# Three pacing constants of a two-layer perceiver: first layers, context sums and routed experts

## The chip, the cores and the metric

The kernel runs on one core of a Trainium2 chip. The metric is the device time of one execution in microseconds; the median of three runs stands for a kernel. One further execution was taken with the hardware profiler, and all views of the trace are of that one. The engines are called by the names of the profile: PE is the matrix engine, PEld its weight loads, DVE the vector engine, ACT the scalar engine, POOL the general engine, SP the engine whose queue issues most DMAs.

## The reference

32 sequences of 64 rows and 256 columns (`x`) attend to 32 contexts of 1601 rows and 256 columns (`ctx_1024`). All arithmetic is float32 but for a ternary last stage.

```python
# first layer
x = x + layernorm(x) @ W1.T + (sum of ctx over its rows) @ W2.T / 1601 + b
x = x + self_attention(layernorm(x))            # 16 heads, a slope bias, 64 x 64 scores
x = x + moe(layernorm(x))                       # shared silu-gated part, and routed experts:
    # routing over all 2048 rows; the rows that routing picks come from flat_idx, and the
    # routed results are added at out[flat_idx], which names only rows 0 to 7
# second layer
x = x + cross_attention(layernorm(x), ctx)      # 16 heads, 64 queries, 1601 keys
x = x + recurrent_block(layernorm(x))           # conv, gated scan, silu-gated part
x = x + ternary_mlp(layernorm(x))
```

`flat_idx` holds expert numbers, so that the routed experts change only eight rows of the first tile, but their counts and groups depend on the routing of all rows.

## The kernel before

The 2048 rows are 16 tiles of 128 rows (two sequences each). They are taken in the order 1 to 15, then 0; `pos` is the place in that order. The cross attention is the backbone: a tile has four halves (two sequences by two groups of 128 channels), and a half four **pieces** of 384 keys (the last has 449). There are 256 pieces, `t` = 0 to 255, and every one issues the same operations in the same order: `column_scores` (L705, the PE products into `s`, then the exponentials into `pt` on ACT), `values` of the next half (`vps` on PE, copied to `vau` on DVE, L667), other work at **place 0**, `row_scores` (L671: products into `r` on PE, the two maxima into `mx` on DVE, L685), `weighted` (L744), `keys` (`kps`), other work at **place 1**. `s` and `r` share one pool of two PSUM tiles, so the products into `s` of the next piece wait until DVE has reduced `r` of this one. All other products go through `mm_tile` (L69), three PSUM tiles in rotation.

Everything else is written as generators that issue a few instructions and yield. A list `plan` (L1128 to L1139) says when each advances; engines then execute in the order of issue, and no scheduler changes it. An entry is `Steps(gen, t0, t1, n, place)`: `n` steps are spread evenly from piece `t0` to piece `t1`, by the rule

```python
while self.gen is not None and self.done * (self.t1 - self.t0) <= (now - self.t0) * self.n:
    self.step()
```

With place 0 the steps run at place 0; with place 2 at both, where place 1 counts as half a piece later; with place 3 at most one step runs in a piece, at place 0 if the step before it ended on ACT's work and else at place 1. At `t1` what is left runs at once. The entries are:

- `first_layer(pos)` (`layer0`, L253): 25 steps, at most one a piece, so about 25 pieces. Step 4 is the first product's input, 8 the query and key products (`q`, `k`), 10 the scores, 11 to 14 the softmax, 16 to 19 the attention's output, 22 to 24 the shared gated part (`su`, `sv`, `so`). It ends in `x3`, the residue, and a column of `logits`.
- `sums(pos, 3)` (`context_sums`, L241): four loads of half a context (`part`, one buffer, SP's queue) and a sum over each on ACT (L236). Three steps lie between a load and its sum, 17 steps in all.
- `queried(pos)` (`query`, L619): the queries of the cross attention, from `x3`.
- `second_layer(pos - 1)` (recurrent block and ternary part): 33 steps from piece `16 * pos + 1` on. Two of them are under way at any time.
- `last_routed()` (`routed`, L423): 78 steps at both places. Step 1 to 3 is the softmax of `logits`; 4 to 7 rank the groups and 8 to 11 the experts (`ranks`, L451, DVE alone: lines L461 to L469); 12 and 13 select and count (`r_cnt`, with one product `cnt_ps`); 14 to 22 load the expert weights and gather the eight rows (`a_ps`, `asb`); 23 to 71 run through eight groups of 512 assignments, each by six steps: DVE makes `ohw` (L561), PE transposes it into `tpo` (L566) and ACT copies that to `ohT` (L568), PE makes `gps` (L574), twice, with a gate on ACT and DVE (`hr`, L229 to L232), and PE adds up `h_ps` (L582); 72 to 78 produce the eight rows.

The routed experts need the logits of all tiles, so they start after the last first layer, and `queried(15)` needs their result: it starts at 229. Half 60, the first of the last tile, has its row scores from piece 235 on. After piece 255 the rest of the last two second layers runs without any backbone.

Of the kernel before, what the change touches and what calls it, by code (L numbers as in the profile page):

```python
# [9 lines left out]
F32 = mybir.dt.float32  # L10
# [5 lines left out]
P = 128  # L16
NB = 32
S = 64
D = 256
# [25 lines left out]
def perceiver_kernel(ctx: ExitStack, tc: tile.TileContext, a: dict, out: bass.AP):  # L45
# [4 lines left out]
    work = ctx.enter_context(tc.tile_pool(name="work", bufs=2))  # L50
# [170 lines left out]
    def mm2(o, lhsT, rhs):  # L221

        for c in range(2):
            nc.tensor.matmul(o, lhsT=lhsT(c), rhs=rhs(c), start=(c == 0), stop=(c == 1))  # L224
# [16 lines left out]
    def context_sums(ti, wait):  # L241

        csum = sums_tile(ti)
        for b in range(2):
            for c in range(2):
                part = load_part(2 * ti + b, c)
                for _ in range(wait):
                    yield
                summed(ti, csum, b, c, part, part)
                yield  # L250
        return csum

    def layer0(ti, csum, k=0, soon=False):  # L253
# [160 lines left out]
        yield  # L414
        o = mm_tile([P, D], f"so_{ti}")
        mm2(o, lambda c: m[:, c, :], lambda c: w_s2[:, c, :])
        x3 = work.tile([P, D], F32, tag="x3", name=f"x3_{ti}", bufs=3)
        nc.vector.tensor_tensor(x3, o, x, ALU.add)
        yield
        return x3  # L420
# [659 lines left out]
    x3, x4, csums = {}, {}, {}  # L1080

    def sums(pos, wait):
        csums[pos] = yield from context_sums(order[pos], wait)

    def first_layer(pos, k=0):
        x3[pos] = yield from layer0(order[pos], csums[pos], k)

    def queried(pos):
        yield from query(pos, x3[pos])

    def second_layer(pos):
        yield from tail(order[pos], x4[pos])

    def last_routed():
        yield from routed(x3[NT - 1])

    def first():

        csum = sums_tile(order[0])
        steps = layer0(order[0], csum, 0, True)  # L1100
        next(steps)
        yield
        next(steps)
        yield
        next(steps)
        junk = big.tile([P, L], F32, tag="part", name="junk", bufs=1)
        for b in range(2):
            yield
            summed(order[0], csum, b, 0, ctxs[b][:, 0, :], junk)
            nc.vector.tensor_reduce(csum[:, 1, b:b + 1], ctxs[b][:, 1, :], AX.X, ALU.add)  # L1110
        csums[0] = csum
        yield
        x3[0] = yield from steps
        yield from query(0, x3[0])
# [13 lines left out]
    plan = [Steps(first_layer(2), 0, 14, 26, 2)]  # L1128
    for pos in range(1, NT):
        if pos > 2:  # L1130
            t0 = 15 * (pos - 3) + 2 + 4 * (pos == 3)
            plan.append(Steps(first_layer(pos), t0, t0 + 28 - 4 * (pos == 3), 28, 3))
            if pos > 3:
                plan.append(Steps(sums(pos, 3), t0 - 16, t0 - 1, 17, 0))
        if pos < NT - 1:
            plan.append(Steps(queried(pos), 16 * (pos - 1) + 2, 16 * (pos - 1) + 10, 6, 0))
        plan.append(Steps(second_layer(pos - 1), 16 * pos + 1, 16 * pos + 30, 33, 3))
    plan.append(Steps(last_routed(), 210, 229, 78, 2))
    plan.append(Steps(queried(NT - 1), 229, 234, 6, 2))  # L1139

    ET = mybir.EngineType
    with tc.manual_schedule(engines={ET.PE, ET.DVE, ET.Activation, ET.Pool}):
# [40 lines left out]
        for h in range(4 * NT):  # L1183
            pos, q = divmod(h, 4)
# [77 lines left out]
```

## Time and profile before

| What | Value |
|---|---|
| median of three runs | 2245.73 us (2244.09 to 2249.22) |
| the profiled execution | 2246.56 us |
| its span, first to last instruction | 2244.8 us |
| PE busy | 2116.0 us, 94% |
| PEld busy | 1563.1 us, 70% |
| DVE busy | 1370.1 us, 61% |
| ACT busy | 933.5 us, 42% |
| POOL busy | 325.8 us, 15% |
| mean granted clock of PE | 0.973 |
| HBM read | 117.70 MB, 53 GB/s over the span |

The span is the time between the first and last instruction of the profiled execution; 1.8 us of its 2246.56 us lie around it. A piece is found in the trace by the products of line L714, the first of its column scores: piece 0 starts at 110.69 us, piece 212 at 1799.78 us, piece 255 at 2165.28 us. A view of waits says which engine stood, on what, and for how long in total; a view of windows gives the busy time of each engine in a stretch and the clock that PE was granted in it, 1.00 being full speed.

### The profile page before, as it was taken

The page shows a single profiled execution, that of the slowest core. Times are in us where ns is not written, and L with a number is a line of the kernel's source. Part 1 is how long each engine was busy: PE and PEld are TensorE (multiplying, and loading weights), DVE is VectorE, ACT ScalarE, POOL GpSimd, SP SyncE. Part 2 cuts the span into 40 slices and gives each one's busy share as a digit, 9 for nine tenths or more (in the row PEclk, how much of TensorE's full clock was granted, in tenths as well). Part 3 has the DMA queues.
Part 4 walks back from the last instruction along what each step waited for, and adds up shares of the span by engine and source line. Part 5 has one row for each costly group of instructions (what it writes and reads, how often), then busy time and mean ns, then how long its engine had stood idle before and what let it go on. Part 6 is the DMA issues. An engine that isn't in the chain of part 4 may idle for free. (4 is left out here: it accounts for less than half of the span.)

```text
span 2244.8 us, 70681 instructions
## 1 busy us (share of the span) xinstructions
PE 2116.0 (94%) x32015; PEld 1563.1 (70%) x32031; DVE 1370.1 (61%) x2926; ACT 933.5 (42%) x1653; POOL 325.8 (15%) x545
## 2 busy tenths in 40 slices
PE   5799999999999999999999999999999988899984
PEld 3476677777677777777776777777777756677763
DVE  3466665666656666665656566665665676666554
ACT  3343444453535444444544444454434313334341
POOL 4111111111111111111111111111110100000011
PEclk8699999999999999999999999999999999999996
DMA  7322111011111111111111101111010011010000
GB/s 240 125 100 96 63 60 63 31 66 47 62 63 61 65 61 36 52 60 60 65 61 63 54 29 63 60 65 46 31 43 30 16 49 40 4 41 34 2 4 5
DMA packets 34763, 124.32 MB, mean 55 GB/s; under 512 B 3218, under 2 KB 16546, under 8 KB 34464
## 3 DMA queue, kind: packets, MB, share of 16 engines
q1 hardware_dynamic: 32608, 115.02, 14.8%
q8 instruction: 251, 4.11, 0.7%
q0 software_dynamic: 1296, 3.97, 0.5%
q10 hardware_dynamic: 560, 0.81, 0.1%
q14 instruction: 48, 0.39, 0.1%
HBM read 117.70 MB, written 2.10 MB: 53 GB/s over the span
## 5 line engine op out<-in xcount | busy, mean ns | idle before, releaser
L685 DVE TENSOR_REDUCE mx<-r 128x2 f32<-128x768 f32 (+1 forms) x512 | 483.8, 986 | 117.1 <-PE r L682 115.9
L726 ACT ACTIVATE pt<-s 128x768 f32<-128x768 f32 x512 | 393.6, 808 | 300.3 <-PE s L721 300.2
L224 PE MATMUL vps<-w_L_xattn_WvT,ctxT 128*128 128x128 f32 (+1 forms) x3328 | 443.8, 285 | 0.0
L650 ACT ACTIVATE kt<-kps,chv 128x384 f32<-128x384 f32 (+1 forms) x256 | 152.1, 594 | 673.7 <-PE kps L224 673.6
L224 PE MATMUL kps<-ctxT,w_L_xattn_WkT 128*128 128x384 f32 (+1 forms) x1024 | 415.3, 529 | 10.8 <-DMA ctxT<-ctxT 10.8
L224 PEld LDWEIGHTS vps<-w_L_xattn_WvT,ctxT 128*128 128x128 f32 (+1 forms) x3328 | 392.1, 189 | 31.1 <-issue 1.0
L667 DVE COPY vau<-vps 128x384 f32<-128x384 f32 (+1 forms) x320 | 154.5, 499 | 378.3 <-PE vps L224 378.0
L744 PEld LDWEIGHTS o<-pt,vau 128*32 128x32 f32 x12288 | 183.9, 110 | 147.7 <-issue 143.7
L682 PE MATMUL r<-kt,qbd 32*128 32x384 f32 (+1 forms) x2048 | 260.9, 552 | 3.2 <-DVE mx L685 1.6
L224 PEld LDWEIGHTS kps<-ctxT,w_L_xattn_WkT 128*128 128x128 f32 x1024 | 175.4, 191 | 111.2 <-issue 37.7
L721 PE MATMUL s<-qbd,kt 32*128 32x128 f32 x6656 | 234.2, 271 | 0.0
L744 PE MATMUL o<-pt,vau 128*32 128x64 f32 x12288 | 225.9, 221 | 2.5 <-ACT pt L726 2.5
L721 PEld LDWEIGHTS s<-qbd,kt 32*128 32x128 f32 x6656 | 222.0, 183 | 4.2
L682 PEld LDWEIGHTS r<-kt,qbd 32*128 32x128 f32 x2048 | 90.1, 184 | 50.4 <-issue 20.6
L714 PEld LDWEIGHTS <-onesb 3*128 3x128 bf16 x1024 | 28.5, 91 | 130.0 <-issue 127.8
L714 PE MATMUL s<-neg,onesb 3*128 3x384 bf16 (+1 forms) x1024 | 98.0, 345 | 17.4 <-DVE mx L685 17.3
L236 ACT ACTIVATE part<-part 128x1601 f32<-128x1601 f32 x60 | 92.5, 1542 | 7.5 <-DMA part<-ctxT 7.5
L761 DVE RECIPROCAL rs<-sums 128x128 f32<-128x128 f32 x64 | 60.6, 947 | 0.1
L302 POOL TENSOR_TENSOR kbd<-kT,mask 128x512 f32<-128x512 f32 x32 | 32.8, 1046 | 155.0 <-ACT kT L295 155.0
L224 PE MATMUL ff<-nT,w_fg 128*128 128x128 f32 x384 | 51.9, 287 | 1.0 <-ACT nT L873 1.0
L908 POOL TENSOR_SCALAR q_i<-h 128x1024 bf16<-128x1024 f32 x16 | 16.7, 1044 | 241.5 <-DVE h L905 189.6
L348 POOL TENSOR_TENSOR s<-s,mx 128x1024 f32<-128x1024 f32 x15 | 28.5, 1903 | 154.8 <-DVE mx L332 145.2
(342 smaller groups left out, 2501.3 us busy)
## 6 DMA issues: line engine op xcount, KB each, us to landing
ctxT<-ctxT SPq DMA_DIRECT2D x32, 1601.0 KB, 6.6
part<-ctxT SPq DMA_DIRECT2D x60, 800.5 KB, 4.4
x<-x SPq DMA_DIRECT2D x16, 128.0 KB, 3.6
out<-x SPq DMA_DIRECT2D x16, 128.0 KB, 1.7
w<-w SPq DMA_DIRECT2D x16, 128.0 KB, 2.2
sum_L_ffn_w1T<-L_ffn_w1T SPq DMA_DIRECT2D x4, 256.0 KB, 4.6
raw_L_ffn_w1T<-L_ffn_w1T SPq DMA_DIRECT2D x4, 256.0 KB, 3.8
sum_L_ffn_w2T<-L_ffn_w2T SPq DMA_DIRECT2D x4, 256.0 KB, 2.6
```

Source lines behind the costliest of these rows:

```text
L224: nc.tensor.matmul(o, lhsT=lhsT(c), rhs=rhs(c), start=(c == 0), stop=(c == 1))
L236: nc.scalar.activation(junk, src, AF.Copy, accum_out=csum[:, c, b:b + 1])
L302: nc.gpsimd.tensor_tensor(kbd[oc], kT[:, oc, :].rearrange("p (b k) -> p b k", b=2).unsqueeze(2).to_broadcast([P, 2, 4, S]), mask4.unsqueez ...
L650: nc.scalar.activation(kt[:, :n], o[:, :n], AF.Identity, bias=chv[:, hf.oc, BK2:BK2 + 1])
L667: nc.vector.tensor_copy(v[:kr, j0:j0 + n, 0:VW - 16].rearrange("p k (h d) -> p k h d", d=17)[:, :, :, 0:16], o[:kr, j0:j0 + n, :].rearrang ...
L682: nc.tensor.matmul(ps[i // 2][:, i % 2, :n], lhsT=qbd[r, hf.oc, hf.b].rearrange("p h q -> p (h q)"), rhs=hf.kt[k][r, :n], start=True, stop ...
L685: nc.vector.tensor_reduce(hf.mx[:, 2 * m:2 * m + 2, k], ps[m][:, :, :n], AX.X, ALU.max)
L714: nc.tensor.matmul(ps[i // 2][:, i % 2, :n * P], lhsT=onesb[r, :], rhs=hf.neg[r, :].unsqueeze(1).to_broadcast([3, n, P]), start=True, stop ...
L721: nc.tensor.matmul(ps[i // 2][:kr, i % 2, j * P:(j + 1) * P], lhsT=hf.kt[g][r, k0:k0 + kr], rhs=qbd[r, hf.oc, hf.b].rearrange("p h q -> p ...
L726: nc.scalar.activation(pt.rearrange("p i k c -> p i (k c)"), ps[m][:, :, :3 * P], AF.Exp)
L744: nc.tensor.matmul(hf.o[32 * c:32 * c + 32, m, :], lhsT=v[:kr, j, 17 * hd:17 * hd + 32], rhs=hf.pt[m][j][:kr, c // 2, c % 2 * S:c % 2 * S ...
L761: nc.vector.reciprocal(rs, t)
```

## The change

First layers start 14 pieces apart in place of 15. The sums of a tile take the 13 pieces before its first layer, but start at piece 7 at the earliest (for the fifth tile, `pos` 4, that is 7 to 15 in place of 1 to 16). The routed experts take the pieces 199 to 229 in place of 210 to 229. `x3` gets a fourth buffer. The first layer of `pos` 15 thereby starts at piece 170 in place of 182. No instruction is added or taken away.

```diff
-        x3 = work.tile([P, D], F32, tag="x3", name=f"x3_{ti}", bufs=3)
+        x3 = work.tile([P, D], F32, tag="x3", name=f"x3_{ti}", bufs=4)
...
-            t0 = 15 * (pos - 3) + 2 + 4 * (pos == 3)
+            t0 = 14 * (pos - 3) + 2 + 4 * (pos == 3)
             plan.append(Steps(first_layer(pos), t0, t0 + 28 - 4 * (pos == 3), 28, 3))
             if pos > 3:
-                plan.append(Steps(sums(pos, 3), t0 - 16, t0 - 1, 17, 0))
+                plan.append(Steps(sums(pos, 3), max(t0 - 14, 7), t0 - 1, 17, 0))
         if pos < NT - 1:
             plan.append(Steps(queried(pos), 16 * (pos - 1) + 2, 16 * (pos - 1) + 10, 6, 0))
         plan.append(Steps(second_layer(pos - 1), 16 * pos + 1, 16 * pos + 30, 33, 3))
-    plan.append(Steps(last_routed(), 210, 229, 78, 2))
+    plan.append(Steps(last_routed(), 199, 229, 78, 2))
     plan.append(Steps(queried(NT - 1), 229, 234, 6, 2))
```

## The prediction

> **What bounds the kernel now.** I read the page first, then windows over stretches of the backbone, then PE's waits in the stretches with holes, then windows of single pieces.
>
> ```profile
> PE 2116.0 (94%) x32015; PEld 1563.1 (70%) x32031; DVE 1370.1 (61%) x2926; ACT 933.5 (42%) x1653; POOL 325.8 (15%) x545
> ...
> PE   5799999999999999999999999999999988899984
> ```
>
> PE is busy nearly throughout, but for the start, the end, and three slices in the routed experts' stretch. The change keeps every instruction, so PE's work stays; only its holes, and time at a lowered clock, can move. Windows cut at piece starts (columns: PE, PEld, DVE, ACT and POOL busy, then granted clock, DMA share, GB/s):
>
> ```profile
> core 0: us, PE busy (x) PEld busy (x) DVE busy (x) ACT busy (x) POOL busy (x), PEclk, DMA share, GB/s
> 1783.18:1829.03 45.85, 35.81 (x488) 26.73 (x488) 38.66 (x107) 12.04 (x24) 3.62 (x10) 0.89 0.11 38
> ...
> 1852.36:1979.55 127.19, 114.59 (x1540) 81.81 (x1540) 78.81 (x175) 46.64 (x87) 8.23 (x16) 0.99 0.09 33
> ...
> 2003.73:2048.94 45.21, 44.81 (x713) 32.27 (x714) 29.34 (x70) 20.36 (x36) 3.28 (x7) 1.00 0.11 38
> 2083.59:2113.76 30.17, 30.17 (x484) 22.74 (x484) 15.54 (x30) 11.58 (x22) 2.31 (x5) 1.00 0.01 2
> ...
> 285.58:1783.18 1497.60, 1481.32 (x23311) 1101.64 (x23319) 938.67 (x1974) 668.98 (x1185) 222.63 (x356) 1.00 0.15 53
> ```
>
> The first row is pieces 210 to 213 (routed steps 1 to 13), the second 216 to 227 (the eight groups). The third is pieces 231 to 236 and the fourth 242 to 245: backbone and two second layers alone. The last, 180 pieces with first layers, has 16.3 us of hole in 1497.6. So what is to be had lies in the routed experts: 10.0 us of hole and 0.11 x 45.85 = 5.0 us of clock in the first row, 12.6 us of hole and about 1.7 of clock in the second. PE's waits in these two stretches:
>
> ```profile
> PE s L714 <- DVE mx L685: 7.9, 4, 6.0
> PE cnt_ps L503 <- DVE r_cnt L501: 2.1, 1, 2.1
> ```
>
> ```profile
> PE tpo L566 <- DVE ohw L561: 6.7, 5, 1.6
> PE gps L574 <- ACT ohT L568: 2.1, 3, 0.8
> PE h_ps L582 <- DVE hr L232: 2.1, 2, 1.8
> ```
>
> The first is DVE overloaded: rank operations are queued ahead of `mx`, and the next piece waits. The second is latency: a step's PE instruction waits for what the step just before it gave to DVE or ACT.
>
> **The eight groups (a gain).** Before, 78 steps over 19 pieces are 2.05 steps a place: after place j (0 at piece 210) `floor(2.0526 j) + 1` steps are done. So two steps share nearly every place. Which pairs share follows from the rule: up to step 37 an even step and the next (24-25, 28-29, 30-31, 34-35, 36-37), from 39 on an odd one and the next (41-42, 47-48, 53-54, 59-60, 65-66). In a group, `ohw` is made in step 23+6g, `tpo` in 24+6g, `gps` in 25+6g, the last `hr` in 28+6g, `h_ps` in 29+6g. That gives three shared `tpo`-`gps`, two shared `hr`-`h_ps` and five shared `ohw`-`tpo`: just the counts 3, 2 and 5 of the waits. The stalls are thus pairs, at 1.34, 0.7 and 1.05 us.
>
> After, 2.6 steps a piece give `floor(1.3 j) + 1`, and three places in ten hold two: (35,36), (48,49), (52,53), (65,66), (70,71) among the groups. Two are `ohw`-`tpo` (2.7 us), one `tpo`-`gps` (0.7), two `hr`-`h_ps` (2.3 with the odd 0.6 us one that this view also has): 5.7 us. Before, with three smaller waits (0.7, 0.6, 0.4), it was 12.2-12.6. **Gain 6.5.** The clock fell to 0.67 over 1882.82 to 1888.00, behind the 1.76 us wait for `hr`, 1.7 us; one such wait has an even chance of coming again: **gain 0.9**. Bounds for the two together: 3 (all pairs that remain cost the longest wait) and 12.
>
> **The ranking (no gain).** Steps 1 to 14 move from pieces 210-213 to 199-204, six pieces in place of four. I had expected more room there, but the phases of the second layers repeat every 16 pieces, and 199-204 has the phases of 231-236, the third row. Free DVE time there is 45.2 - 29.3 = 15.9 us; in 242-245, the phases of 210-213, it is 30.2 - 15.5 = 14.6 us. The routed steps added 38.66 - 15.54 = 23.1 us of DVE, and step 14 (clearing and filling `r_z`) 1.6. Overflow before 8.5, after 54.0 - 45.2 = 8.8. The single pieces 232 to 236, below a row of before's stall:
>
> ```profile
> 1812.59:1819.30 6.71, 6.34 (x52) 5.71 (x52) 6.37 (x16) 1.51 (x2) 0.00 (x0) 0.58 0.00 1
> ...
> 2014.06:2020.78 6.72, 6.72 (x108) 4.92 (x108) 6.51 (x17) 2.09 (x3) 0.87 (x2) 1.00 0.01 2
> 2020.78:2026.82 6.04, 6.04 (x104) 4.11 (x105) 4.07 (x11) 2.29 (x5) 2.40 (x5) 1.00 0.01 4
> 2026.82:2033.42 6.60, 6.55 (x105) 4.25 (x106) 2.72 (x4) 4.70 (x6) 0.00 (x0) 1.00 0.00 0
> 2033.42:2041.55 8.13, 7.82 (x133) 5.32 (x134) 5.22 (x13) 4.41 (x8) 0.00 (x0) 1.00 0.48 168
> 2041.55:2048.94 7.39, 7.35 (x120) 5.30 (x120) 4.76 (x12) 3.29 (x7) 0.00 (x0) 1.00 0.10 41
> ```
>
> Piece 200 (like 232) has DVE full already: `mx` ends 0.6 us ahead of the next piece. Step 3 (1.8 us of DVE) at its place 0 makes a stall of 1.2. Step 4 (1.4) is carried over, 201 takes steps 5 and 6 (2.8) ahead of `mx`: its copy of `vau` ends 2.3 us late, stall 2.9. 202 takes step 7 (1.4) and 8 (3.2): 1.8. Steps 9 and 10 (6.1) at its place 1 delay the copy of `vau` in 203, step 11 (3.1) follows ahead of `mx`: 5.1. In 204, step 12 (1.3), the round trip of `cnt_ps` (PE waits 2.5), and steps 13 and 14 ahead of `mx`: 2.2. Together 15.7. Each of the five stalls on `mx` ends some 0.5 us sooner, since the first scores need only the first of two reductions: 13.2. Before it was 10.0. **Loss 3.2**; bounds -5 (a gain: the overflow spread evenly, 8.8 less what is left over at the end) and 6.
>
> Here a rule speaks for the change: the Trainium skill, Perfetto Trace Analysis, section Optimization Strategy, says that stretches with different contended engines may gain by being interleaved. By it all 29 us of holes and clock would go, and the time be about 2217. But the rows show DVE's free time equal in both places. I take the rows.
>
> **The clock.** The row 1812.59 to 1819.30 was granted 0.58, after the 6.04 us wait, and 1819.30 to 1829.03 got 0.82 behind one of 2.14. The Trainium skill, TensorE: Matmul & The Clock Gate, Part 1, lets the clock halve after about 3.4 us of idleness. By that only the stall of 5.1 would lower it, 1.7 to 3.4 us lost; by the rows stalls from 1.8 us on can, up to 8. While DVE is the bound part of the loss hides under the waits for it. I take 3 (before 5.0), **gain 2**, bounds 0 lost to 8.
>
> **First layers 14 apart (about nothing).** Summed from the groups by line over 600 to 1500 us, a first layer brings some 11 us of DVE and 14 of PE: it brings more PE time than DVE time, so packing it denser does not overload DVE. What is new is that step 22 of one layer and step 8 of the next share place 0: `su`, `sv`, `k` and `q` ask for four PSUM tiles out of three. `q` waits until `su` is read; PE needs 2.1 us for `sv` and `k`, ACT's tanh and DVE's copy 0.8 after `su`. Covered; if DVE is behind, the nearest row is `su` waiting 0.7 us for a tile. I take **0.5 us** in all, bounds -2 and 15 (eleven pairs at 1.4). POOL (15% busy) takes its part of the moved steps under cover.
>
> **Sums, loads, `x3` (nothing).** Each tile's four loads (800.5 KB, 4.4 us to land) stay three steps ahead of their sums: 2.3 pieces, some 18 us, in place of 2.6; for `pos` 4 two pieces, 14 us. On SP's queue they pass the context loads (6.6 us to land), still inside. If a load came late, ACT would stand, and `pt` and PE behind it, at most a few us per tile. The routed weights (2.2 us to land) are loaded two steps ahead, now one and a half places rather than one. At most three `x3` live at a time in either kernel, so the fourth buffer ends no wait. After piece 229 nothing moves.
>
> **The sum.** -6.5 - 0.9 + 3.2 - 2.0 + 0.5 = -5.7. From the profiled 2246.56 that is 2240.9; the median stands 0.83 below that execution, so 2240.0.
>
> **The rivals.** *A, the holes vanish*: spreading lets DVE catch up between pieces, as it has slack in the mean (45.2 against 29.3). Then 10.0 + 5.0 of the ranking mostly go besides the 7.4 of the groups: -22, 2224. Against it: the full row of piece 232, and that steps come in pairs just at the ranks (9, 10). *B, PSUM at the eleven joint places*: `q` and `k` wait for `su` and `vps` behind a DVE that still copies `vau`. At 1.3 us per tile, +14 on the -5.7: 2254. It decides from 0.5 us per tile on. For it: `su` already waits 0.7 us for a tile here and there; against it: in 1497.6 us all waits make 16.3. *C, the change does little*: the groups' pairs cost more than counted and the ranking takes the gain: -1, 2245.
>
> **How the numbers follow.** A measurement of this kernel can tell about 0.2%, 4.5 us, from no change. The likeliest case with C in its upper part has 0.55, range 2233 to 2247: faster 0.32, same 0.22, slower 0.01. A has 0.2, all faster. B has 0.25: slower 0.22, same 0.03. The range 2226 to 2254 leaves out the lower part of A and the upper of B; faster and slower both being open, the likeliest case's own range is 2233 to 2247.
>
> **What would show it.** PE's waits of `tpo`, `gps` and `h_ps` should be 2, 1 and 2 times, some 5.5 us. `mx` should hold up `s` in pieces 200 to 204, 8 to 13 us, with a clock below 1 there. Pieces 205 to 228 should be nearly without holes. PE's hole before piece 199 should stay near 16 us per 1500. Waits of `q`, `k`, `su` or `so` at 0.5 us and more, a dozen of them, would be B; no wait on `mx` about piece 203 would be A; a wait on a DMA of `part` would refute the cover of the sums.

## The result and the profile after

| Kernel | median, us | ratio to before | 95% interval |
|---|---|---|---|
| before | 2246.13 | | |
| changed | 2250.02 | 1.0019 | 1.0012 to 1.0026 |

The change makes the kernel 3.9 us slower (2250.02 - 2246.13, 20 runs of each), 0.19%, clear of the noise. The profiled execution of the changed kernel took 2253.73 us, at the upper side of its runs: the rest from piece 252 on, the same instructions in both kernels, took 93.7 us in it at a mean granted clock of 0.71, and 91.1 us at 0.74 in that of before. So stretches of the backbone are compared here, not spans. First the page of the changed kernel:

```profile
span 2251.7 us, 70663 instructions
...
PE 2122.3 (94%) x32015; PEld 1566.7 (70%) x32031; DVE 1369.0 (61%) x2926; ACT 934.3 (41%) x1653; POOL 327.1 (15%) x545
...
PE   5799999999999999999999999999999899999984
```

The three weak slices of the routed experts have become one. PE, PEld, DVE, ACT and POOL have the same numbers of instructions as before. The windows of the changed kernel, cut at its own piece starts (PE, PEld, DVE, ACT and POOL busy, granted clock, DMA share, GB/s), are in this order pieces 16 to 194, 199 to 204 (the ranking), 205 to 209, 207 to 227 (the eight groups), and 0 to 251, the whole backbone up to its last half:

```profile
236.06:1681.23 1445.17, 1423.05 (x22290) 1057.34 (x22296) 906.96 (x1902) 646.07 (x1142) 226.26 (x357) 1.00 0.16 54
...
1712.62:1773.94 61.32, 49.06 (x705) 34.66 (x706) 50.75 (x147) 20.92 (x37) 3.84 (x10) 0.94 0.08 28
1773.94:1821.87 47.93, 47.40 (x608) 33.14 (x609) 25.93 (x50) 13.25 (x22) 3.14 (x5) 0.93 0.17 48
1796.33:1985.36 189.03, 183.30 (x2639) 133.00 (x2640) 116.83 (x258) 70.48 (x132) 14.10 (x27) 1.00 0.10 34
111.24:2157.99 2046.75, 1999.68 (x31051) 1476.52 (x31066) 1280.25 (x2731) 876.10 (x1546) 276.75 (x448) 1.00 0.15 51
```

The same for before, first pieces 16 to 194 and then the whole backbone:

```profile
235.52:1666.72 1431.20, 1414.93 (x22221) 1051.84 (x22229) 901.95 (x1890) 642.93 (x1136) 223.24 (x354) 1.00 0.16 54
...
110.69:2153.69 2043.00, 1996.36 (x31051) 1475.14 (x31064) 1281.27 (x2731) 875.25 (x1546) 275.54 (x448) 0.99 0.15 51
```

The backbone is 3.75 us longer (2046.75 - 2043.00), about what the medians say. In pieces 16 to 194 PE's holes (length less busy) grew from 16.3 to 22.1 us. In the ranking they are 12.3 us, 10.0 before; in the groups 5.7, 12.6 before. So the holes shrank in the routed part and grew under the first layers, and over the whole backbone they about cancel: 47.1 us, 46.6 before. The other 3.3 us of the loss are PE busy time (1999.68 - 1996.36), with the same instructions and a mean granted clock of 1.00 (0.99 before). Which part of the change costs them, the windows don't tell; the runs below do.

### The profile page after: what moved, and what is told of

Read it like the earlier page. It is cut to its first block, busy times and chain, and to the rows that moved or that the text cites. A ratio compares the mean times of both kernels' runs of the same rounds, so it can differ in the third digit from the quotient of the medians.

```text
span 2251.7 us, 70663 instructions
## 1 busy us (share of the span) xinstructions
PE 2122.3 (94%) x32015; PEld 1566.7 (70%) x32031; DVE 1369.0 (61%) x2926; ACT 934.3 (41%) x1653; POOL 327.1 (15%) x545
## 4 chain that ended last, share of the span: by engine, by line
PE 84%; DVE 9%; ACT 3%; issue 2%; POOL 1%; SPq 1%; DMA 0%; POOLq 0%; DVEq 0%; ACTq 0%
PE vps L224 17%; PE kps L224 16%; PE r L682 9%; PE o L744 9%; PE s L721 8%; PE ff L224 4%; PE s L714 3%; DVE mx L685 2%; PE ffo L886 2%; PE q L224 1%; PE wo L778 1%; PE hg L837 1%; ACT pt L726 1%; DVE vau L667 1%; PE su L224 1%
## 5 line engine op out<-in xcount | busy, mean ns | idle before, releaser
L714 PE MATMUL s<-neg,onesb 3*128 3x384 bf16 (+1 forms) x1024 | 98.0, 345 | 16.4 <-DVE mx L685 16.2
```

The lines of the kernel that those rows point to most:

```text
L714: nc.tensor.matmul(ps[i // 2][:, i % 2, :n * P], lhsT=onesb[r, :], rhs=hf.neg[r, :].unsqueeze(1).to_broadcast([3, n, P]), start=True, stop ...
```

## The experiments

All ratios are to runs of the kernel before on the same chip. The theory after reading the two traces: closer first layers cost PE some 7 to 10 us, because two transposes of a first layer now stand behind a layer ahead of it and wait for a PSUM tile; the longer routed stretch gives part of it back. Rivals: the ranking's new place costs the time (1), the bunched sums do (2). Rivals 3 to 5 came up on the way and are named in the expectations of the runs that bear on them. In brackets behind a time stand its ratio and the 95% interval.

### The spacing alone, and the sums alone

```diff
 # e1_spacing, on the changed kernel
-    plan.append(Steps(last_routed(), 199, 229, 78, 2))
+    plan.append(Steps(last_routed(), 210, 229, 78, 2))
 # e2_sums, on the kernel before
-                plan.append(Steps(sums(pos, 3), t0 - 16, t0 - 1, 17, 0))
+                plan.append(Steps(sums(pos, 3), max(t0 - 14, 7), t0 - 1, 17, 0))
...
-        x3 = work.tile([P, D], F32, tag="x3", name=f"x3_{ti}", bufs=3)
+        x3 = work.tile([P, D], F32, tag="x3", name=f"x3_{ti}", bufs=4)
```

> The changed kernel with the routed experts put back to pieces 210 to 229; first layers 14 apart, sums in 13. Theory (the first layers' closer spacing costs some 7 us in PE holes ahead of piece 199, the longer routed stretch gives 3 to 4 back): 2253, that is 7 above before, with the same holes ahead of piece 199 as in the changed kernel and those of before in 210 to 229. Rival 1 (the spacing is free, the ranking in pieces 199 to 204 costs the time): 2246, as before.

> The kernel before with two parts of the change alone: sums in 13 pieces (7 at the earliest) and the fourth buffer of x3; first layers stay 15 apart, routed experts 210 to 229. Theory: 2246, nothing, with holes ahead of piece 199 as before. Rival 2 (sums bunched on ACT hold the PSUM tiles that tp_b waits for): 2250 to 2253.

Measured: `e1_spacing` 2257.30 us (1.0042, 1.0030 to 1.0054), 4 us more than expected; `e2_sums` 2246.77 us (1.0002, 0.9993 to 1.0012). The whole backbone of `e1_spacing`:

```profile
110.08:2162.94 2052.86, 2001.46 (x31066) 1475.20 (x31066) 1281.77 (x2731) 875.36 (x1546) 276.06 (x448) 1.00 0.15 50
```

The spacing alone costs 9.9 us of backbone (2052.86 - 2043.00), more than the whole change; by the medians on that chip it is 10.0 (2257.30 - 2247.28). Sums and `x3` cost nothing. Rivals 1 and 2 fall as the cause.

### The steps that wait for a PSUM tile

What `tp_b` (step 7 of a first layer) waits for in pieces 16 to 194, before and then in the changed kernel (releaser, us in total, times):

```profile
L208 PE MATMUL tp_b<-ident,xn_b x24: 272/273/330, 292.2 to 1618.1; 128*128 128x128 f32 x24
its engine sat idle before it (us, times) until:
  ACT oT L379: 0.5, 1
```

```profile
L208 PE MATMUL tp_b<-ident,xn_b x24: 272/273/332, 282.6 to 1534.0; 128*128 128x128 f32 x24
its engine sat idle before it (us, times) until:
  DVE vau L667: 1.6, 7
  ACT h L929: 1.0, 1
  DVE rr L842: 0.6, 1
  ACT oT L379: 0.5, 1
```

None of these makes `xn_b`, which `tp_b` transposes; all are readers of PSUM tiles. One case, piece 92 of the changed kernel (start, duration, engine, line):

```profile
847.45 0.41 DVE L190 TENSOR_SCALAR xn_b<-x,mv_b,rstd_b 128x256 f32<-128x256 f32 x1
...
849.21 1.61 PE L837 MATMUL hg<-nT,w_hg 64*96 64x128 f32 x16
...
850.74 0.44 PE L208 MATMUL tp_c<-ident,xn_c 128*128 128x128 f32 x2
...
851.33 0.97 DVE L842 TENSOR_SCALAR rr<-hg 96x256 f32<-96x256 f32 x2 [0.49 <-ACT zz L841]
...
851.81 0.44 PE L208 MATMUL tp_b<-ident,xn_b 128*128 128x128 f32 x2 [0.63 <-DVE rr L842]
```

`xn_b` is there from 847.86 on (847.45 + 0.41). But `hg` of a second layer takes two of the three tiles and `tp_c`, step 21 of the layer ahead, the third; `tp_b` waits until DVE has read the first `hg`. At 14 pieces step 7 meets step 21, at 15 it met step 22. Likewise step 4 (`tp_a`) meets step 18. A plain `yield` in place of `yield ACT` puts the next step at place 1 of the piece; that takes the meeting away and leaves the spacing:

```diff
 # e3_tpb, on the changed kernel (e5_before_tpb: the same on the kernel before)
         xn = normalised(tile_([P, D], "xn", "xn_b"), m)
-        yield ACT
+        yield
 # e13_spacing_places: e1_spacing with this, and the same behind xn_a
         xn = normalised(tile_([P, D], "xn", "xn_a"), m)
-        yield ACT
+        yield
```

> The changed kernel with one yield of the first layer changed from ACT to plain, after xn_b: step 7 (the transposes tp_b and their copy xT_b) then runs at place 1 and no longer behind the tp_c of the layer ahead at place 0. Theory (tp_b waits for a PSUM tile that tp_c and values left no place for): the 5 us that tp_b lost go, 2245. Rival 1 and 2: 2250, as the changed kernel.

> The kernel before with the one yield after xn_b changed as in e3_tpb, nothing else. Theory (at 15 pieces step 7 shares place 0 with step 22 of the layer ahead, and tp_b hardly waited: 0.6 us ahead of piece 199): 2246, within 2 us of before. Rival 3 (step 7 at place 1 is better at any spacing): 2241.

> e1_spacing (first layers 14 apart, routed experts 210 to 229) with step 4 and step 7 of the first layer at place 1. Theory (these two steps' waits for a PSUM tile are nearly all of the 10 us that the spacing costs): 2247 to 2249, level with before to within 2 us. Rival (they are only what the profile shows as their waits, 5 us; the rest is the closer spacing itself): 2252.

Measured: `e3_tpb` 2241.58 us (0.9976, 0.9967 to 0.9985), more than expected; `e5_before_tpb` 2247.28 us (1.0002, 0.9994 to 1.0010), nothing, as the theory has it; `e13_spacing_places` 2245.95 us (0.9995, 0.9987 to 1.0003), level with before as the theory has it. Rival 3 falls. Pieces 16 to 194 of `e1_spacing`, of `e3_tpb` and of `e13_spacing_places`:

```profile
234.91:1679.99 1445.08, 1423.52 (x22300) 1057.31 (x22296) 906.63 (x1902) 645.37 (x1142) 226.33 (x357) 1.00 0.16 54
```

```profile
237.21:1676.62 1439.41, 1421.63 (x22300) 1058.40 (x22297) 906.35 (x1902) 644.60 (x1142) 226.32 (x357) 1.00 0.16 54
```

```profile
234.51:1670.85 1436.34, 1420.12 (x22300) 1059.48 (x22297) 907.03 (x1902) 643.55 (x1142) 224.97 (x357) 1.00 0.16 54
```

The same work takes 5.7 us less with `tp_b` moved and 8.7 less with both. Of the 8.7, 5.3 are holes (21.6 to 16.2); 3.4 are PE busy time, which fell from 1423.52 to 1420.12 with the same number of matmuls. So a wait costs more than the hole that the trace shows for it. The trace shows where the 3.4 us lie. If PE time is counted only where no earlier product covers it, the 24 products of `tp_b` take 4.8 us in `e1_spacing` and 2.6 in `e13_spacing_places`, those of `tp_a` 4.6 and 2.6, though one lasts a median of 0.27 to 0.28 us in both: a transpose behind a wait no longer runs under the products ahead of it. These 4.1 us, less 0.7 elsewhere, are the 3.4; the holes ahead of these two steps (3.8 and 1.6 us in `e1_spacing`, none in `e13_spacing_places`) are the 5.3. The cost of the spacing is the meeting of steps, not the density. That the PSUM tile is what they wait for rests on the releasers and on cases such as piece 92; no run gives the pool a fourth tile.

The other part of what `e3_tpb` gained lies behind the first layers. Pieces 195 to 229, with the same steps, took 317.4 us in it and 320.6 in the changed kernel; in `e1_spacing` and `e13_spacing_places` they took 326.8 and 322.8. Much of this is the granted clock (1.00 over pieces 205 to 209 of `e3_tpb`, 0.93 in the changed kernel). So a difference of less than some 4 us between single profiles of the routed stretch shows nothing by itself.

### The place and the rate of the routed experts

```diff
 # e4_early19, on the changed kernel
-    plan.append(Steps(last_routed(), 199, 229, 78, 2))
+    plan.append(Steps(last_routed(), 199, 218, 78, 2))
 # e11_late22, on the kernel before
-    plan.append(Steps(last_routed(), 210, 229, 78, 2))
+    plan.append(Steps(last_routed(), 207, 229, 78, 2))
 # e12_from195_only, on the changed kernel
-    plan.append(Steps(last_routed(), 199, 229, 78, 2))
+    plan.append(Steps(last_routed(), 195, 229, 78, 2))
```

> The changed kernel with the routed experts over pieces 199 to 218, 19 as before but at the early place. Theory (spreading takes away the pairs of dependent steps, 9 to 10 us, while the early place of the ranking costs 5 to 7): pairs and their waits of tpo, gps, h_ps come back as before (6.7, 2.1, 2.1 us), the ranking overflows more: 2260 to 2264. Rival 1 (place alone counts, not the rate): 2250.

> The kernel before with the routed experts alone changed, from piece 207 (the first after its last first layer) to 229, 22 pieces instead of 19; first layers 15 apart. Theory (at 1.77 steps a place all ten dependent pairs still share a place by the rule, so the groups gain nothing; the ranking has a little more room, 3 us): 2243. Rival 5 (any longer stretch gains in proportion, 11 us over 11 pieces): 2243 as well for 3 pieces, but then with shorter waits of tpo.

> The changed kernel with the routed experts from piece 195 instead of 199 and nothing else. Theory: 2250 less 8 for the routed part, 2242; the holes ahead of 195 as in the changed kernel. Difference to e9_from195: the 7 to 8 us of the first layers.

Measured: `e4_early19` 2262.21 us (1.0069, 1.0053 to 1.0084), as expected; `e11_late22` 2246.62 us (0.9999, 0.9992 to 1.0006) and `e12_from195_only` 2252.33 us (1.0017, 1.0006 to 1.0028), both misses, by 4 and 10 us: a longer stretch alone did nothing that the medians show. (By the backbone of its profile `e12_from195_only` is 3.7 us shorter than the changed kernel, 2043.1 against 2046.8.) The four longest of PE's waits in the routed stretch of `e4_early19` (us in total, times, longest):

```profile
PE s L714 <- DVE mx L685: 8.9, 4, 5.2
PE tpo L566 <- DVE ohw L561: 8.2, 5, 2.4
PE cnt_ps L503 <- DVE r_cnt L501: 3.0, 1, 3.0
PE gps L574 <- ACT ohT L568: 2.5, 3, 1.1
```

With 19 pieces the pairs are back, five `tpo` and three `gps`; 1.6 us more went to a load of routed weights that had not landed. Against `e1_spacing` (same spacing, same rate, other place) the early place costs 0.27% by the ratios, 6 us; against the changed kernel (same place) the rate is worth 0.50%, 11 us. In `e11_late22` the ranking came to lie in 208 to 211. PE's waits in the groups fell by 3.1 us (9.1 against 12.2), those in the ranking rose by 3.1 (13.1 against 10.0), and most of these were one:

```profile
PE cnt_ps L503 <- DVE r_cnt L501: 8.8, 1, 8.8
```

### The rank steps apart

If what the ranking lacks is not a longer stretch but distance between four steps of 3.1 us, an empty step after each should help; that makes 82 steps:

```diff
 # e6_ranks, on the changed kernel
                 nc.vector.tensor_reduce(rk[:, r], gt, AX.X, ALU.add)
                 yield
+                if kept is not None:
+                    yield
...
-    plan.append(Steps(last_routed(), 199, 229, 78, 2))
+    plan.append(Steps(last_routed(), 199, 229, 82, 2))
 # e7_tpb_ranks: with the yield of e3_tpb; e8_all: with that behind xn_a too
```

> The changed kernel with an empty step after each of the four expert-rank steps and 82 steps in place of 78 over the same 30 pieces. Theory (in pieces 199 to 209 DVE overflows because four rank steps of 3.1 us fall into 1.5 pieces; in three pieces they fit better): the 12.8 us of hole and 6.8 us of clock in 199 to 209 fall to some 12 together, 2243. Rival 4 (the overflow is set by DVE's free time over the whole stretch, wherever the rank steps lie): 2249 to 2250.

> Both edits, that of e3_tpb and that of e6_ranks, on the changed kernel. Theory: the two stretches are apart, so the gains add up: 2235. If they have one cause after all: 2240.

> e7_tpb_ranks with the yield after xn_a changed as well, so that step 4 (tp_a) runs at place 1 and no longer behind step 18 of the layer ahead at place 0. Theory: tp_a lost 1.8 us more than before by the same cause as tp_b, and these go: 2 us below e7_tpb_ranks. If tp_a only moves its wait to step 5's product: the same as e7_tpb_ranks.

Measured: `e6_ranks` 2247.24 us (1.0006, 0.9998 to 1.0013), `e7_tpb_ranks` 2244.20 us (0.9990, 0.9982 to 0.9998), `e8_all` 2242.86 us (0.9984, 0.9978 to 0.9991). The first two are misses, by 4 and 9 us; `e8_all` is 1.3 us below `e7_tpb_ranks`, where 2 were expected. Pieces 199 to 204 of `e6_ranks` are 8.1 us shorter than the changed kernel's, with the clock at 1.00:

```profile
1712.29:1765.51 53.22, 45.39 (x704) 31.89 (x704) 45.48 (x127) 20.79 (x37) 3.68 (x9) 1.00 0.09 32
```

But its pieces 210 to 229 are 6.1 us longer (186.0 against 179.9), 3.1 of them holes. And `e7_tpb_ranks` is above `e3_tpb`, not 6 us below it. Its pieces 199 to 209 are shorter by 3.8 us (102.4 against 106.1), its pieces 210 to 229 longer by 7.4 (187.3 against 179.9), of which 3.1 are holes and most of the rest is 6.8 us at half clock. With 82 steps in 30 pieces seven dependent pairs of the groups share a place, by the rule that spreads the steps, and not five. The rate moves two things at once. By the ratios the two moved steps are worth only 0.22%, 4.9 us, from `e6_ranks` to `e8_all`, though pieces 16 to 194 became 8.7 us shorter: the routed stretch (pieces 195 to 229) of `e8_all` is 4.0 us longer with the same steps, at a lower clock (0.97 against 0.99).

### A rate without pairs

From piece 195, the first after the last first layer, 82 steps over 34 pieces leave no dependent pair in one place by the rule; 78 steps leave two.

```diff
 # e9_from195, on the changed kernel: both yields of the first layer plain, and
+    plan.append(Steps(last_routed(), 195, 229, 78, 2))
 # e10_from195_ranks: e8_all, and
+    plan.append(Steps(last_routed(), 195, 229, 82, 2))
 # e14_ranks195: e10_from195_ranks with the two yields of the first layer as before
```

> The changed kernel with step 4 and step 7 of the first layer at place 1 (the yields after xn_a and xn_b plain) and the routed experts from piece 195 instead of 199, 78 steps over 34 pieces. Theory (rate of 1.15 a place leaves two shared pairs of dependent steps instead of five, and the rank steps fall into 198 to 200, half of them singly): ahead of 195 as e8_all, 195 to 229 some 8 us less of hole and clock than the changed kernel has in 199 to 229; 2234. Rival 4 (only DVE's free time counts, and 34 pieces have the same share of it): 2239.

> As e9_from195 with the empty step after each expert-rank step, 82 steps over 34 pieces: by the rule that spreads the steps, no dependent pair of the groups shares a place, and no rank step shares a piece with another for long. Theory: the groups without waits of tpo, gps and h_ps, the ranking with 5 us of hole at most; 2231. If the pairs were not the cause: as e9_from195.

> e10_from195_ranks without the two moved steps of the first layer: the changed kernel with the routed experts from piece 195 in 82 steps, an empty one after each expert rank. Theory (the two parts are apart and add up): 9 us above e10_from195_ranks, 2235. Rival (the gain of e10_from195_ranks needs the moved steps): 2245.

Measured: `e9_from195` 2240.27 us (0.9974, 0.9963 to 0.9985), 6 us above what was expected; `e10_from195_ranks` 2226.15 us (0.9912, 0.9899 to 0.9925), 5 us below; `e14_ranks195` 2234.75 us (0.9952, 0.9938 to 0.9965). `e10_from195_ranks` is 20 us faster than before, and its distance to `e14_ranks195`, 8.6 us, is that of the two moved steps, as expected: here the parts add up. `e9_from195` alone would have spoken for rival 4 (2239), but `e10_from195_ranks`, with the same DVE work in the same stretch, refutes it. Pieces 199 to 204 of `e9_from195`, then of `e10_from195_ranks`:

```profile
1703.32:1771.59 68.27, 57.16 (x736) 38.93 (x736) 48.76 (x122) 20.35 (x36) 3.57 (x9) 0.90 0.15 49
```

```profile
1706.75:1762.55 55.80, 50.17 (x720) 35.07 (x720) 44.41 (x112) 19.41 (x34) 3.71 (x8) 0.97 0.15 50
```

In `e9_from195` the four rank steps still fall within 1.5 pieces: 11 us of hole and a clock of 0.90. With the empty steps these six pieces are 12.5 us shorter, but some work has moved out of them (736 matmuls against 720). Over pieces 195 to 209, with 1824 and 1819 matmuls, the gain is 9.0 us (142.4 against 133.4); pieces 210 to 229, without pairs, give 3.8 more (176.1 against 172.3). All that PE still waited for from piece 195 to 229 in `e10_from195_ranks`:

```profile
PE s L716 <- DVE mx L687: 7.9, 9, 2.0
PE tpo L568 <- DVE neg L705: 0.7, 1, 0.7
PE a_ps L542 <- PE tp_f L208: 0.6, 1, 0.6
PE cnt_ps L505 <- DVE r_cnt L503: 0.4, 1, 0.4
```

No wait on `ohw`, `ohT` or `hr` is left, as the rule for the pairs had it.

## Why the prediction was wrong

It said 2240.0 us, faster; the kernel is 3.9 us slower, within the range but on the other side. The step that failed is "First layers 14 apart (about nothing)". It took 0.5 us, bounds -2 and 15; `e1_spacing` measured 9.9 by the backbone. It looked for the meeting at place 0 between steps 22 and 8 and found `q` covered, and that was right: `q` did not wait once in pieces 16 to 194 of the changed kernel. But it looked at the one meeting with the most PE work and took the others to cost nothing. Steps 21 and 7, two tiny transposes, meet too, as do 18 and 4, and what counts is not PE time but how many of three PSUM tiles are out; in piece 92, with a second layer's `hg` beside them, there are four. Moving steps 4 and 7 alone took the 9.9 us back (`e13_spacing_places`, 0.9995). Rival B had the kind of cause, PSUM tiles at joint places, and set it at 14 us, but on `q` and `k`, and with only a quarter of the chance. That all waits of the stretch made only 16.3 us was no argument against it: they were those of a spacing at which these steps don't meet.

The rest, point by point:

- **The groups**: right in sum. Two `tpo`, one `gps` and two `hr`-`h_ps` meetings were forecast, 5.7 us. The waits of the changed kernel in pieces 207 to 227:

```profile
PE tpo L566 <- DVE ohw L561: 3.5, 3, 1.7
PE gps L574 <- ACT ohT L568: 0.8, 1, 0.8
PE h_ps L582 <- DVE neg L703: 0.7, 1, 0.7
```

  With three of 0.2 us these are 5.6. Two of the three on `tpo` are of 1.6 us and more; the pairs on `hr` hardly waited (2.3 us were forecast for them), and `tpo` waited 0.8 us more than forecast, so the close sum is in part luck.
- **The ranking**: right in sign and about in size. 13.2 us of stall were forecast, in pieces 200 to 204; there are 12.3:

```profile
PE s L714 <- DVE mx L685: 8.6, 9, 2.3
PE cnt_ps L503 <- DVE r_cnt L501: 2.1, 1, 2.1
PE kps L224 <- DVE vau L667: 1.6, 1, 1.6
```

  They are more even than in the working: no wait is over 2.3 us, where 5.1 was expected for piece 203. The wait of `kps` for `vau` is the PSUM tile that DVE held while it ranked. That spreading the ranking over more pieces would not make room was right; the 2217 of the general rule was further off. The runs add what the argument lacked: the rank steps must lie apart from each other, not only in a longer stretch (`e10_from195_ranks` against `e9_from195`).
- **The clock**: 3 us were taken; the two windows at 0.94 and 0.93 lost 0.06 x 61.3 + 0.07 x 47.9 = 7.0, against 5.0 before. Here the rows were the better guide: waits of no more than 2.3 us lowered it, so that the 3.4 us of idleness of the Trainium skill's rule (TensorE: Matmul & The Clock Gate, Part 1) are not needed in this case. The gain of 2 was a loss of 2. In the groups the clock stayed at 1.00, so that the 1.7 us lost there before were gained, where 0.9 were taken.
- **The routed part in sum**: -6.2 us were forecast (-6.5, -0.9, +3.2, -2.0). From `e1_spacing` to the changed kernel the backbone fell by 6.1 (2052.86 - 2046.75). By the ratios of the two it is 0.23%, 5.2 us. The errors in the parts offset one another, and profiles of this stretch differ by up to 4 us for the same steps, so the agreement to 0.1 us is luck.
- **Sums, loads, `x3`**: right, `e2_sums` is level.
- **Rival A**, that the holes vanish, was wrong for this rate and place, and can nearly be made right: over pieces 195 to 233 PE's holes are 10.0 us in `e10_from195_ranks`, 24.5 before.

So the change is +9.9 from the closer spacing, by the meetings of two steps, and -6.1 from the earlier and slower routed steps, +3.8 by the backbone, +3.9 by the medians.

## What to carry to other kernels

When hand-paced streams share a small rotation of PSUM tiles, a new spacing is a new set of meetings: list for it which steps share a place and count the tiles they hold, transposes too, and don't ask only where the busy time is. A spreading rule decides which dependent steps are issued back to back, so choose the rate by the pairs that it makes, and set heavy steps of one engine apart by empty ones; 82 steps over 34 pieces, which did both, were worth 14 us over 78 steps there, from 2240.27 to 2226.15. A part of a change that is "about nothing" deserves its own run before anything else: the spacing alone would have told the sign.

## What the runs showed of the hardware

- A short wait costs more than its hole. Moving the two steps took 5.3 us of hole and 3.4 us of PE busy time out of pieces 16 to 194, with the same instructions, and in three other pairs of runs these pieces became shorter by 8.7 to 8.9 us as well (`e6_ranks` to `e8_all`, `e12_from195_only` to `e9_from195`, `e14_ranks195` to `e10_from195_ranks`). The busy time lies in the waiting transposes themselves, which overlap the products ahead of them less: 4.8 and 4.6 us not covered, in place of 2.6 each.
- The granted clock fell to 0.93 over pieces 205 to 209 of the changed kernel, with 0.5 us of hole in them: in the 6.8 us from 1774.46 on it was 0.50, with PE busy for 6.5 of them. The waits in the pieces before were of at most 2.3 us. The lowered clock comes after the wait and falls on full pieces.
- The last stretch (from piece 252 on) holds the same instructions in every kernel here, and took 89.7 us (`e3_tpb`, granted clock 0.75) to 94.2 us (`e1_spacing`, 0.71). PE's holes in it are nearly the same in all, 37.9 to 38.7 us. In this serial end with long waits the clock alone scatters the time by over 4 us, as much as this change moves.
